# Two of Linear's four blocks turned by block loads and VectorE in place of TensorE, and the order of their pieces

## The chip, the cores and the metric

One core of one Trainium2 chip runs the whole program in one launch. The metric is the device time in microseconds (us) of that launch. The program is bound to one order of instructions on each of its engines when it is built: TensorE (PE in the profile) multiplies, VectorE (DVE), ScalarE (ACT) and GpSimd (POOL) work on elements, and SyncE (SP) issues nearly all transfers between HBM and the on-chip SBUF, one after the other. Engines wait for one another on semaphores; an engine takes its instructions strictly in order, so what waits holds all that stands behind it.

## What is computed

The input `x` has 2 sequences of 1024 tokens, 512 wide, in float32. Four layers follow, each with a residual and a layernorm after it:

```python
x = _layernorm(x + _L0_attn_ref(x, ...))   # Mamba-like recurrent layer, inner width 1024
x = _layernorm(x + _L0_ffn_ref(x, ...))    # ternary linear layer, here called Linear
x = _layernorm(x + _L1_attn_ref(x, ...))   # gated linear recurrence (RG-LRU) with a short convolution
x = _layernorm(x + _L1_ffn_ref(x, ...))    # SwiGLU with weights stored as integers
```

The change lies in the second layer, at its border with the first and the third:

```python
out = jnp.einsum('bln,nk->blk', x, weight) * scale      # weight is -1, 0 or 1
v_norm = jnp.maximum(jnp.linalg.norm(out, axis=-1, keepdims=True), EPS)
out = out * (jnp.tanh(v_norm) / (v_norm + EPS))
o_norm = jnp.maximum(jnp.linalg.norm(out, axis=-1, keepdims=True), EPS)
out = out * jnp.minimum(0.99 / o_norm, 1.0)
```

## The kernel before

The 2048 tokens are cut into four blocks of 512 (`NBLK = 4`, `TB = 512`), and a block's rows into four tiles of 128 tokens (`NJ = 4`); the 512 features are four tiles of 128 as well (`NK = 4`). A block in rows, tokens on the partitions, is `X[b]`; each layer's products want it turned, features on the partitions. Line numbers are those of the kernel before.

The first layer works block by block. Its last step for a block is `conclude`: for each row tile `j` eight matmuls `po` (L770, in two halves of four, each 128x128 by 128x512 in float32) give the output rows, and VectorE adds them, times `rms`, to `X[b]` (L785, printed `x<-po,rms,x`). The `rms` come from sums of squares that `gate` makes before: ACT squares (L757), and POOL adds seven of them up into `sums` (L759). The squares live in temporary buffers of the first layer's pool, which is given back when they are done with. The finished blocks are normalised and stored to HBM in rows as `x_mid[b]`, blocks 0 to 2 well before the stretch that matters here, and block 3 inside it.

`later_layers` opens two pools in the space that the first layer gives back: `ep` (tiles of the second and fourth layer) and `wp` (the third layer's weights, tags w0 to w4). A tile that takes space over from others waits for whoever last used that space. Then it issues its loads on SP, in this order: `w_f0` (Linear's weight, L900), `X[0]` and `X[1]` in rows from `x_mid` (L903), Linear's scale (L99), `w_x` and `w_y` (L909), `X[2]` (L910), the parameters (L93, L861), and later `w_ig`, `w_ag` and the fourth layer's integer weights (L927).

`linear(b)` is a generator that does the Linear layer for block `b`, in four steps divided by `yield`:

1. turn the block and split it in two parts, a rounded one and the rest (`split`), so that the product with the ternary weight is exact in TensorE's fast format. Blocks 0, 1 and 2 are turned by `transposed`: sixteen PE transposes (L237) into four PSUM banks, ACT's cast (L241) of each bank and DVE's subtraction (L244). Block 3 (`mid`) is turned by `load_blocks` and `turn_blocks`: four DMAs (L265) bring `x_mid[3]` from HBM in pieces of 32 floats, placed so that 32x32 blocks only have to be transposed in themselves, and DVE does that with four instructions (L273), after which ACT casts (L955) and DVE subtracts (L957).
2. eight matmuls (L987, four features by two parts) for each of two row tiles, and for each DVE's multiplication by the scale into `o` (L991) and ACT's sum of squares (L993);
3. the same for the other two row tiles;
4. the tail: ACT and DVE make the factor `f` from the norms (L997 to L1009), DVE adds `o` times `f` to the rows (L1011, `x<-o,f,x`), takes the layernorm's statistics (L283, L286, reciprocal L289), and POOL normalises the rows (L291; for block 0 DVE takes the last of the four rows). Blocks 1 to 3 are stored as `x_lin[b]`.

The order around it is made by `weave(main, fill, plan)`, which takes `plan[i]` steps of `fill` after step `i` of `main`. conclude of block 3 has eight steps, two for each row tile, and a last one with its layernorm and store; linear(0) and linear(1) are its fill:

```python
weave(steps, itertools.chain(linear(0), linear(1)), (0, 1, 0, 2, 0, 1, 0, 2, 1))
```

Then comes the third layer. `branches(0)` turns the finished `x0` with sixteen PE transposes (L237, evicted by ACT at L249 into a tile in slot w4) and multiplies it with `w_x` and `w_y` (L1069); linear(2) is woven into it with `(1,) * 4`, and linear(3) into the gates that follow. From there the third layer and the fourth run as before and after.

The tile framework has a scheduler: within what the data and the buffers allow, it may move an instruction in its engine's order by priority. `tc.keep_in_program_order(...)` holds one instruction behind the one that was written just before it on its engine; others may still be moved past either.

`parameters()` also computes a softplus of `a_param` on DVE and ACT (L213 to L224), some twenty small instructions on 128x4 elements which the scheduler strews between others.

Of the kernel before, what the change touches and what calls it, by code (L numbers as in the profile page):

```python
# [9 lines left out]
F32 = mybir.dt.float32  # L10
# [3 lines left out]
ALU = mybir.AluOpType  # L14
PSUM = bass.MemoryType.PSUM

P = 128
TB = 512
NJ = TB // P
D = 512  # L20
NK = D // P
# [16 lines left out]
def model_kernel(ctx: ExitStack, tc: tile.TileContext, t: dict, out: bass.AP):  # L38
    nc = tc.nc
    ctx.enter_context(nc.allow_non_contiguous_dma(reason="small parameter columns"))  # L40
    BATCH, SEQ, _ = t["L0_attn_hidden_states"].shape
    NBLK = BATCH * SEQ // TB
# [3 lines left out]
    x_mid = tc.dram_tile([NBLK, TB, D], F32, name="x_mid")  # L46
# [35 lines left out]
    X = [tokens() for _ in range(3)]  # L82
# [49 lines left out]
    w_out = op.tile([P, NX, D], F32, tag="w_out", name="w_out")  # L132
# [90 lines left out]
        nc.vector.tensor_scalar(r, z, 0.0, None, ALU.max)  # L223
        nc.vector.scalar_tensor_tensor(o, p, 2.0, r, ALU.mult, ALU.add)  # L224

    def transposed(pool, b, X, tags=("xT",), split=False, bufs=1, by_act=False, behind=False, soon=False):


        pieces = [
            pool.tile([P, NK, TB], F32R if split else F32, tag=tag, name=f"{tag}{b}", bufs=bufs)  # L230
            for tag in tags
        ]
        xT = pieces[0]
        for k in range(NK):
            pt = bank("pt")
            for j in range(NJ):
                nc.tensor.transpose(  # L237
                    pt[:, j * P : (j + 1) * P], X[b][:, j, k * P : (k + 1) * P], ident
                )
            if split:  # L240
                copied = nc.scalar.copy(xT[:, k, :], pt)  # L241
                if behind:
                    tc.keep_in_program_order(copied)
                nc.vector.tensor_tensor(  # L244
                    pieces[1][:, k, :], pt, xT[:, k, :].bitcast(F32), ALU.subtract
                )
            elif soon:
                with tc.high_priority():
                    nc.scalar.copy(xT[:, k, :], pt)  # L249
            elif k % 2 or by_act:  # L250
                nc.scalar.copy(xT[:, k, :], pt)
            else:
                nc.vector.tensor_copy(xT[:, k, :], pt)
        return pieces
# [6 lines left out]
    def load_blocks(dst, rows, pinned=False):  # L261

        blocks = rows.rearrange("(n t) (k a c) -> a t k n c", t=32, k=NK, c=32)
        for a in range(4):
            load = nc.sync.dma_start(  # L265
                dst[32 * a : 32 * a + 32].rearrange("t k (n c) -> t k n c", c=32), blocks[a]
            )
            if pinned:
                tc.keep_in_program_order(load)

    def turn_blocks(dst, src=None, pinned=False):
        for k in range(NK):
            turned = nc.vector.transpose(dst[:, k, :], (src or dst)[:, k, :])  # L273
            if pinned:
                tc.keep_in_program_order(turned)
# [28 lines left out]
    def weave(main, fill, plan, rest=True):  # L304

        for i, _ in enumerate(main):
            for _ in range(plan[i] if i < len(plan) else 0):
                next(fill, None)
        for _ in fill if rest else ():
            pass  # L310
# [451 lines left out]
    def conclude(b, st):  # L762


        xc, sums = st["xc"], st["sums"]
        rms = sp.tile([P, NJ], F32, tag="rms", name="rms")
        for j in range(NJ):
            po = bank("po")
            for m in range(NX):
                nc.tensor.matmul(  # L770
                    po, xc[:, m, j * P : (j + 1) * P], w_out[:, m, :],
                    start=(m == 0), stop=(m == NX - 1),
                )
                if m == NX // 2 - 1:
                    yield
            if j == 0:
                pss = bank("pss")
                for i in range(NJ):
                    nc.tensor.matmul(
                        pss[:, i : i + 1], sums[:, i * P : (i + 1) * P], ones,  # L780
                        start=True, stop=True,
                    )
                nc.scalar.activation(rms, pss[:, :NJ], AF.Sqrt, bias=eps, scale=1.0 / DI)
                nc.vector.reciprocal(rms, rms)
            nc.vector.scalar_tensor_tensor(  # L785
                X[b][:, j, :], po, rms[:, j : j + 1], X[b][:, j, :], ALU.mult, ALU.add
            )
            yield
        if b:
            layernorm(X[b], pinned=b == NBLK - 1)  # L790
            store_rows(x_mid[b], X[b])
# [93 lines left out]
    def later_layers(exact, last=None):  # L885
# [4 lines left out]
        X = Y  # L890
# [8 lines left out]
        w_f0 = ep.tile([P, NK, D], F32, tag="wF", name="w_f0" + suffix)  # L899
        nc.sync.dma_start(w_f0, w_f0_source)  # L900
        rows_mid = [x_mid[b].rearrange("(j p) d -> p j d", p=P) for b in range(NBLK)]
        for b in range(2):
            nc.sync.dma_start(X[b], rows_mid[b])  # L903
        w1 = [
            wp.tile([P, NK, D], F32, tag=f"w{i}", name=f"w1{i}{suffix}") for i in range(4)
        ]
# [41 lines left out]
            wf = ep.tile([P, NK, D], F32, tag="wg0", name="wfg")  # L948
            nc.vector.tensor_copy(wf, w_f0)

        def split(x, pieces):


            for k in range(NK):
                nc.scalar.copy(pieces[0][:, k, :], x[:, k, :])  # L955
                if exact:
                    nc.vector.tensor_tensor(  # L957
                        pieces[1][:, k, :], x[:, k, :], pieces[0][:, k, :].bitcast(F32),
                        ALU.subtract,
                    )  # L960
# [7 lines left out]
        def linear(b):  # L968

            tags = ("wu0", "wd0") if exact else ("wu0",)  # L970
            if b == NBLK - 1:
                turn_blocks(mid)
                w1.append(wp.tile([P, NK, D], F32, tag="w4", name="w14" + suffix))
                xT = [ep.tile([P, NK, TB], WT, tag=tag, name=f"{tag}{b}") for tag in tags]
                split(mid, xT)
                nc.sync.dma_start(w1[4], w_sources["w_out"])
            else:

                xT = transposed(ep, b, X, tags=tags, split=exact, behind=b == 2)
            yield  # L980
            o = ep.tile([P, NJ, D], F32, tag="wF", name="o" + suffix)
            ssq = sp.tile([P, NJ], F32, tag="ssq", name="ssq")
            for j in range(NJ):
                po = bank("po")
                for k in range(NK):
                    for x in xT:
                        nc.tensor.matmul(  # L987
                            po, x[:, k, j * P : (j + 1) * P], wf[:, k, :],
                            start=(k == 0 and x is xT[0]), stop=(k == NK - 1 and x is xT[-1]),
                        )  # L990
                nc.vector.tensor_tensor(o[:, j, :], po, f0s, ALU.mult)  # L991
                junk = ep.tile([P, GW], mybir.dt.bfloat16, tag="junk", name="junk2")
                nc.scalar.activation(junk, o[:, j, :], AF.Square, accum_out=ssq[:, j : j + 1])  # L993
                if j % 2:
                    yield
            norm = sp.tile([P, NJ], F32, tag="norm", name="norm")
            nc.scalar.activation(norm, ssq, AF.Sqrt)  # L997
            v = sp.tile([P, NJ], F32, tag="v", name="v")
            nc.vector.tensor_scalar(v, norm, 1e-7, None, ALU.max)
            f = sp.tile([P, NJ], F32, tag="f", name="f")  # L1000
            nc.scalar.activation(f, v, AF.Tanh)
            nc.vector.tensor_scalar(v, v, 1e-7, None, ALU.add)
            nc.vector.reciprocal(v, v)
            nc.vector.tensor_tensor(f, f, v, ALU.mult)
            nc.vector.tensor_tensor(norm, norm, f, ALU.mult)
            nc.vector.tensor_scalar(norm, norm, 1e-7, None, ALU.max)
            nc.vector.reciprocal(norm, norm)
            nc.vector.tensor_scalar(norm, norm, 0.99, 1.0, ALU.mult, ALU.min)
            nc.vector.tensor_tensor(f, f, norm, ALU.mult)  # L1009
            for j in range(NJ):  # L1010
                nc.vector.scalar_tensor_tensor(  # L1011
                    X[b][:, j, :], o[:, j, :], f[:, j : j + 1], X[b][:, j, :],
                    ALU.mult, ALU.add,
                )
            layernorm(X[b], engine=nc.gpsimd, last=None if b else nc.vector)
            if b:
                store_rows(x_lin[b], X[b])
            yield

        if last:  # L1020
            steps, free = last

            weave(steps, itertools.chain(linear(0), linear(1)), (0, 1, 0, 2, 0, 1, 0, 2, 1))
            free()
        else:
            for _ in itertools.chain(linear(0), linear(1)):
                pass
        for i, name in ((2, "w_ig"), (3, "w_ag")):
            nc.sync.dma_start(w1[i], w_sources[name])
# [28 lines left out]
        with tc.tile_pool(name="rec" + suffix, bufs=1, side="right", reuse_waits="tile") as rp:  # L1058
# [125 lines left out]
                yield  # L1184

            st = {}
            weave(branches(0, st), linear(2), (1,) * 4)
            lin = [coming_block(1)]
            bout = row("L1_attn_b_out", D, c1, nc.sync, "scale")
            ys = []  # L1190
# [254 lines left out]
```

## Time and profile before

| | us |
|---|---|
| median of 3 runs | 1117.68 |
| lowest and highest | 1117.55, 1117.88 |
| the profiled execution | 1116.89 |
| its span, first to last instruction | 1115.1 |
| PE busy | 1099.4 (99%) |
| DVE busy | 701.4 (63%) |
| ACT busy | 451.4 (40%) |
| POOL busy | 366.8 (33%) |
| PE at conclude's products (L770, 256) | 112.5 |

The granted clock of PE is 0.998 in the mean. "Busy" is time in which an engine has an instruction under way; for PE the ends of the pipelined matmuls are modelled. In lists of the profile a line reads: start, length, engine, line of the kernel, operation, output<-inputs by the program's names, and in brackets how long the engine was idle before it and what ended that. "SPq" is the issue of a transfer in SP's queue, not the transfer. A list of waits reads: who <- what it waited for: us in total, times, longest.

### The profile page before, as it was taken

What the parts mean: (1) busy time and instruction counts of PE and PEld (TensorE: products, weight loads), DVE (VectorE), ACT (ScalarE), POOL (GpSimd) and SP (SyncE); (2) the same over time, 40 slices, a digit from 0 to 9 for tenths busy, and PEclk for the clock granted to TensorE, in tenths of its full rate; (3) what the DMA queues carried; (4) which work ended last, traced back from release to release, by engine and by line L of the source; (5) the groups of instructions that cost most, each with busy time, mean ns of one, the idle gap of its engine ahead of it and who ended that gap; (6) DMA issues with size and microseconds to landing.
All of it is one profiled execution on the core that took longest, in us unless ns stands there. A gap on an engine that the chain in (4) does not pass through costs nothing.

```text
span 1115.1 us, 12073 instructions
## 1 busy us (share of the span) xinstructions
PE 1099.4 (99%) x4450; PEld 663.3 (59%) x4450; DVE 701.4 (63%) x1267; ACT 451.4 (40%) x690; POOL 366.8 (33%) x347
## 2 busy tenths in 40 slices
PE   8999999999999999999999999999999999999996
PEld 5455445445544555745444444447888888888885
DVE  5989797797869676875727437184238866325224
ACT  3334624463454233556653372553223224224223
POOL 1547471565348240254433231236511001001000
PEclk9999999999999999999999999999999999999999
DMA  8005200911210137245650001304544002100001
GB/s 323 21 9 126 91 1 17 253 30 39 105 81 0 39 135 215 57 94 123 113 113 37 1 1 49 27 0 143 189 94 76 1 1 63 14 1 30 8 1 41
DMA packets 122059, 77.04 MB, mean 69 GB/s; under 512 B 94512, under 2 KB 95312, under 8 KB 120456
## 3 DMA queue, kind: packets, MB, share of 16 engines
q1 hardware_dynamic: 120792, 75.77, 25.7%
q8 instruction: 37, 0.61, 0.2%
q10 hardware_dynamic: 976, 0.39, 0.1%
q14 instruction: 30, 0.25, 0.1%
q0 software_dynamic: 224, 0.02, 0.0%
HBM read 59.95 MB, written 16.02 MB: 68 GB/s over the span
## 4 chain that ended last, share of the span: by engine, by line
PE 80%; DVE 11%; ACT 4%; issue 2%; POOL 2%; DMA 1%; SPq 0%; DVEq 0%; ACTq 0%; POOLq 0%
PE pgu L1039 20%; PE p L1069 16%; PE po L1270 10%; PE pg L372 9%; PE px L372 7%; PE po L770 6%; DVE acc L298 3%; PE po L1159 2%; PE py L705 2%; DVE L L578 2%; PE po L987 2%; PE pxt L674 1%; PE pt L237 1%; POOL x L1165 1%; PE py L697 1%
## 5 line engine op out<-in xcount | busy, mean ns | idle before, releaser
L1050 DVE SCALAR_TENSOR_TENSOR h<-pgu,L_ffn_up_scale,sg 128x512 f32<-128x512 f32 x63 | 47.1, 748 | 126.4 <-PE pgu L1039 122.6
L372 PE MATMUL px<-xT,w_in 128*128 128x512 f32 x256 | 114.6, 597 | 0.0
L593 POOL TENSOR_TENSOR L<-L,gm 128x512 f32<-128x512 f32 x64 | 93.5, 1490 | 63.7 <-DVE bdec L588 34.7
L372 PE MATMUL pg<-xT,w_in 128*128 128x512 f32 x256 | 113.5, 594 | 0.0
L770 PE MATMUL po<-w_out,xc 128*128 128x512 f32 x256 | 112.5, 593 | 0.7 <-DVE L L578 0.7
L1069 PE MATMUL p<-cv,w 128*128 128x512 f32 x256 | 110.8, 592 | 0.0
L1039 PE MATMUL pgu<-wF__4239,wg 128*128 128x512 f32 x256 | 101.7, 397 | 0.0
L1039 PE MATMUL pgu<-lo__4240,wg 128*128 128x512 f32 x256 | 100.8, 394 | 0.0
L1039 PE MATMUL pgu<-lo__4240,wu 128*128 128x512 f32 x256 | 100.7, 393 | 0.0
L1039 PE MATMUL pgu<-wF__4239,wu 128*128 128x512 f32 x256 | 100.7, 393 | 0.0
L1270 PE MATMUL po<-wd,hh 128*128 128x512 f32 x252 | 98.3, 396 | 0.3 <-POOL wg L930 0.3
L1270 PE MATMUL po<-wd,hl 128*128 128x512 f32 x252 | 98.3, 396 | 0.2 <-DVE hl L1054 0.2
L1049 ACT ACTIVATE sg<-pgu,L_ffn_gate_scale 128x512 f32<-128x512 f32 x63 | 43.4, 689 | 127.6 <-PE pgu L1039 127.6
L770 PEld LDWEIGHTS po<-w_out,xc 128*128 128x128 f32 x256 | 48.4, 190 | 61.8 <-issue 56.7
L1053 ACT CAST hh<-h 128x512 fp32r<-128x512 f32 x63 | 39.1, 621 | 112.5 <-DVE h L1050 112.3
L1069 PEld LDWEIGHTS p<-cv,w 128*128 128x128 f32 x256 | 48.6, 190 | 60.4 <-issue 58.8
L1069 PE MATMUL p<-xT,w 128*128 128x512 f32 x192 | 82.9, 592 | 0.0
L372 PEld LDWEIGHTS px<-xT,w_in 128*128 128x128 f32 x256 | 47.5, 190 | 57.5 <-issue 55.5
L298 DVE SCALAR_TENSOR_TENSOR acc<-xpad,cols,acc 128x512 f32<-128x512 f32 x72 | 68.5, 953 | 20.0 <-ACT acc L342 15.2
L372 PEld LDWEIGHTS pg<-xT,w_in 128*128 128x128 f32 x256 | 47.3, 190 | 54.2 <-issue 53.1
L1386 POOL TENSOR_TENSOR x<-x,r 128x512 f32<-128x512 f32 x12 | 15.2, 1295 | 195.0 <-DVE r L1385 195.0
L578 DVE TENSOR_TENSOR_SCAN L<-pl,id 128x512 f32<-128x512 f32 x64 | 75.0, 1205 | 4.7 <-ACT pl L572 3.7
(292 smaller groups left out, 1921.9 us busy)
## 6 DMA issues: line engine op xcount, KB each, us to landing
L<-decays SPq DMA_DIRECT2D x12, 1024.0 KB, 8.0
x_mid<-x SPq DMA_DIRECT2D x4, 1024.0 KB, 4.3
x<-x_mid SPq DMA_DIRECT2D x4, 1024.0 KB, 7.5
st<-in_L_ffn_gate_w_dram SPq DMA_DIRECT2D x8, 512.0 KB, 6.4
st<-in_L_ffn_up_w_dram SPq DMA_DIRECT2D x8, 512.0 KB, 4.4
st<-in_L_ffn_down_w_dram SPq DMA_DIRECT2D x8, 512.0 KB, 3.8
x_rec<-x SPq DMA_DIRECT2D x4, 1024.0 KB, 4.3
x<-_attn_hidden_states_dram SPq DMA_DIRECT2D x3, 1024.0 KB, 16.8
```

The costliest lines, as they stand in the source:

```text
L298: tap = nc.vector.scalar_tensor_tensor(acc, xpad[:, k : k + TB], w[:, k : k + 1], acc, ALU.mult, ALU.add)
L372: nc.tensor.matmul(pm[:n, :], w_in[:, k, lo : lo + n], xT[:, k, :], start=(k == 0), stop=(k == NK - 1),)
L578: nc.vector.tensor_tensor_scan(L[:, h, :], pl, id4.rearrange("p j t -> p (j t)"), 0.0, ALU.mult, ALU.add)
L593: nc.gpsimd.tensor_tensor(L[:, h, :], L[:, h, :], st["gm"], ALU.mult)
L705: nc.tensor.matmul(pys[i][hh * HD : (hh + 1) * HD, q, :], dtx[q][:, 2 * i + hh, :], L[:, h, s], start=(first and q == 0), stop=(q == 1), s ...
L770: nc.tensor.matmul(po, xc[:, m, j * P : (j + 1) * P], w_out[:, m, :], start=(m == 0), stop=(m == NX - 1),)
L1039: nc.tensor.matmul(pm, w[g][:, k, cols], x[:, k, :], start=(k == 0 and x is pieces[0]), stop=(k == NK - 1 and x is pieces[-1]),)
L1049: nc.scalar.activation(sg, pgu[0], AF.Silu, scale=gs[:, m : m + 1])
L1050: nc.vector.scalar_tensor_tensor(h, pgu[1], us[:, m : m + 1], sg, ALU.mult, ALU.mult)
L1053: nc.scalar.copy(halves[0], h)
L1069: nc.tensor.matmul(pm, w1[i][:, k, m * P : (m + 1) * P], rhs[:, k, :], start=(k == 0), stop=(k == NK - 1),)
L1270: nc.tensor.matmul(po[j], x[:, j * P : (j + 1) * P], wd[m // GK][:, m % GK, :], start=(m == 0 and x is h[0]), stop=(m == NF - 1 and x is h ...
```

## The change

linear(1) and linear(2) are turned as linear(3) was: two new tiles, `raw1` (in `wp`, tag w4, and the first tile of that pool) and `raw2` (in `ep`, tag lo) are loaded with `load_blocks` from `x_mid[1]` and `x_mid[2]`, turned in place by DVE's `turn_blocks`, and split from SBUF. raw1's four DMAs are issued between `w_f0` and the rows of `X[0]`; raw2's four come after the rows of `X[1]`. The 2 x 16 PE transposes of these blocks go.

The order changes too. `first_two()` interleaves the steps of linear(0) (`one`), linear(1) (`two`) and linear(2) (`third`): the first step of a block stands in front of the last step (the tail) of its neighbour. The first step of linear(2) has a `yield` of its own between the turns and the split. Three steps in place of two are taken after conclude's row tile 1 (the third is linear(1)'s turn and split). linear(2) has its first two steps there (turns and split), and the rest is woven into `branches(0)`, beginning one step later, with `(0, 1, 1, 1)`. Held behind the instruction written before them are: conclude's evictions of row tiles 1 and 2 of the last block, the turns of blocks 1 and 2, the casts of block 2, and the instruction `v` (maximum with 1e-7) of linear(1). The argument `behind` of `transposed` goes.

```diff
@@ -223,7 +223,7 @@
         nc.vector.tensor_scalar(r, z, 0.0, None, ALU.max)
         nc.vector.scalar_tensor_tensor(o, p, 2.0, r, ALU.mult, ALU.add)
 
-    def transposed(pool, b, X, tags=("xT",), split=False, bufs=1, by_act=False, behind=False, soon=False):
+    def transposed(pool, b, X, tags=("xT",), split=False, bufs=1, by_act=False, soon=False):
 
 
         pieces = [
@@ -238,9 +238,7 @@
                     pt[:, j * P : (j + 1) * P], X[b][:, j, k * P : (k + 1) * P], ident
                 )
             if split:
-                copied = nc.scalar.copy(xT[:, k, :], pt)
-                if behind:
-                    tc.keep_in_program_order(copied)
+                nc.scalar.copy(xT[:, k, :], pt)
                 nc.vector.tensor_tensor(
                     pieces[1][:, k, :], pt, xT[:, k, :].bitcast(F32), ALU.subtract
                 )
@@ -782,9 +780,12 @@
                     )
                 nc.scalar.activation(rms, pss[:, :NJ], AF.Sqrt, bias=eps, scale=1.0 / DI)
                 nc.vector.reciprocal(rms, rms)
-            nc.vector.scalar_tensor_tensor(
+            sum_ = nc.vector.scalar_tensor_tensor(
                 X[b][:, j, :], po, rms[:, j : j + 1], X[b][:, j, :], ALU.mult, ALU.add
             )
+            if b == NBLK - 1 and 0 < j < NJ - 1:
+
+                tc.keep_in_program_order(sum_)
             yield
         if b:
             layernorm(X[b], pinned=b == NBLK - 1)
@@ -899,8 +900,17 @@
         w_f0 = ep.tile([P, NK, D], F32, tag="wF", name="w_f0" + suffix)
         nc.sync.dma_start(w_f0, w_f0_source)
         rows_mid = [x_mid[b].rearrange("(j p) d -> p j d", p=P) for b in range(NBLK)]
+
+        def untouched(b, pool, tag):
+
+            x = pool.tile([P, NK, TB], F32, tag=tag, name=f"raw{b}" + suffix)
+            load_blocks(x, x_mid[b])
+            return x
+
+        raw = [untouched(1, wp, "w4")]
         for b in range(2):
             nc.sync.dma_start(X[b], rows_mid[b])
+        raw.append(untouched(2, ep, "lo"))
         w1 = [
             wp.tile([P, NK, D], F32, tag=f"w{i}", name=f"w1{i}{suffix}") for i in range(4)
         ]
@@ -948,11 +958,13 @@
             wf = ep.tile([P, NK, D], F32, tag="wg0", name="wfg")
             nc.vector.tensor_copy(wf, w_f0)
 
-        def split(x, pieces):
+        def split(x, pieces, pinned=False):
 
 
             for k in range(NK):
-                nc.scalar.copy(pieces[0][:, k, :], x[:, k, :])
+                cast = nc.scalar.copy(pieces[0][:, k, :], x[:, k, :])
+                if pinned:
+                    tc.keep_in_program_order(cast)
                 if exact:
                     nc.vector.tensor_tensor(
                         pieces[1][:, k, :], x[:, k, :], pieces[0][:, k, :].bitcast(F32),
@@ -968,15 +980,19 @@
         def linear(b):
 
             tags = ("wu0", "wd0") if exact else ("wu0",)
-            if b == NBLK - 1:
-                turn_blocks(mid)
-                w1.append(wp.tile([P, NK, D], F32, tag="w4", name="w14" + suffix))
+            if b:
+                x = mid if b == NBLK - 1 else raw.pop(0)
+                turn_blocks(x, pinned=b < NBLK - 1)
+                if b == 2:
+                    yield
+                if b == NBLK - 1:
+                    w1.append(wp.tile([P, NK, D], F32, tag="w4", name="w14" + suffix))
                 xT = [ep.tile([P, NK, TB], WT, tag=tag, name=f"{tag}{b}") for tag in tags]
-                split(mid, xT)
-                nc.sync.dma_start(w1[4], w_sources["w_out"])
+                split(x, xT, pinned=b == 2)
+                if b == NBLK - 1:
+                    nc.sync.dma_start(w1[4], w_sources["w_out"])
             else:
-
-                xT = transposed(ep, b, X, tags=tags, split=exact, behind=b == 2)
+                xT = transposed(ep, b, X, tags=tags, split=exact)
             yield
             o = ep.tile([P, NJ, D], F32, tag="wF", name="o" + suffix)
             ssq = sp.tile([P, NJ], F32, tag="ssq", name="ssq")
@@ -996,7 +1012,10 @@
             norm = sp.tile([P, NJ], F32, tag="norm", name="norm")
             nc.scalar.activation(norm, ssq, AF.Sqrt)
             v = sp.tile([P, NJ], F32, tag="v", name="v")
-            nc.vector.tensor_scalar(v, norm, 1e-7, None, ALU.max)
+            least = nc.vector.tensor_scalar(v, norm, 1e-7, None, ALU.max)
+            if b == 1:
+
+                tc.keep_in_program_order(least)
             f = sp.tile([P, NJ], F32, tag="f", name="f")
             nc.scalar.activation(f, v, AF.Tanh)
             nc.vector.tensor_scalar(v, v, 1e-7, None, ALU.add)
@@ -1017,13 +1036,22 @@
                 store_rows(x_lin[b], X[b])
             yield
 
+        third = linear(2)
+
+        def first_two():
+
+            one, two = linear(0), linear(1)
+            for steps in (one, one, one, two, one, third, two, two, third, two):
+                next(steps)
+                yield
+
         if last:
             steps, free = last
 
-            weave(steps, itertools.chain(linear(0), linear(1)), (0, 1, 0, 2, 0, 1, 0, 2, 1))
+            weave(steps, first_two(), (0, 1, 0, 3, 0, 1, 0, 2, 1))
             free()
         else:
-            for _ in itertools.chain(linear(0), linear(1)):
+            for _ in first_two():
                 pass
         for i, name in ((2, "w_ig"), (3, "w_ag")):
             nc.sync.dma_start(w1[i], w_sources[name])
@@ -1184,7 +1212,7 @@
                 yield
 
             st = {}
-            weave(branches(0, st), linear(2), (1,) * 4)
+            weave(branches(0, st), third, (0, 1, 1, 1))
             lin = [coming_block(1)]
             bout = row("L1_attn_b_out", D, c1, nc.sync, "scale")
             ys = []
```

## Prediction

> **What bounds the kernel now.** I read the page's busy shares first, then the chain of waits over the stretch that the change touches (395 to 515 us), then the queues that feed PE there.
>
> ```profile
> PE 1099.4 (99%) x4450; PEld 663.3 (59%) x4450; DVE 701.4 (63%) x1267; ACT 451.4 (40%) x690; POOL 366.8 (33%) x347
> PEclk9999999999999999999999999999999999999999
> ```
>
> PE is busy for 1099.4 of 1115.1 us, at full clock. Work taken from PE is time saved, and any wait put in front of PE is time lost: no idle time is there to absorb it. The chain (start, length, what) through the last conclude and the Linear blocks:
>
> ```profile
> 408.93 6.87 PE po L770 x16
> 415.79 0.79 PE pss L779 x8
> 416.58 1.81 PE pt L237 x16
> 418.38 6.87 PE po L770 x16
> 425.25 7.30 PE po L987 x32
> 432.56 13.73 PE po L770 x32
> 446.29 1.75 PE pt L237 x16
> 448.04 7.47 PE po L987 x32
> 455.51 3.49 PE pt L237 x32
> 459.00 3.44 PE p L1069 x8
> ```
>
> No gap anywhere. L770 is conclude's product, L987 Linear's, L237 the transposes: block 0's at 416.58, block 1's at 446.29, and at 455.51 thirty-two, namely 16 of the finished x0 (branch 0's input) and then 16 of block 2. Two deadlines matter below: PE wants x0's raw rows at 416.58, and x0's finished rows after linear(1), at 455.51.
>
> SP's queue (start, length in the queue, what) shows when the rows come:
>
> ```profile
> 408.96 0.91 SPq L903 DMA_DIRECT2D x<-x_mid  x2
> 409.92 0.50 SPq L99 DMA_DIRECT2D L_ffn_scale<-in_L_ffn_scale_dram  x1
> 415.40 0.37 SPq L909 DMA_DIRECT2D w<-in_L_attn_w_x_dram  x1
> ...
> SPq L903 <- PE pg L372: 6.6, 1, 6.6
> SPq L909 <- POOL sums L759: 5.0, 1, 5.0
> ```
>
> x0 and x1 leave at 408.96. The next big load, w_x into slot w0, waits 5.0 us for conclude's last sums on POOL (L759, seven adds from 404.06, 11.31 us long, to 415.37): that slot lies where the last squares are.
>
> DVE and POOL (same columns) close x0 for its second deadline:
>
> ```profile
> 438.91 0.16 DVE L1009 TENSOR_TENSOR f<-f,norm 128x4 f32<-128x4 f32 x1
> 439.11 0.75 DVE L1011 SCALAR_TENSOR_TENSOR x<-o,f,x 128x512 f32<-128x512 f32 x1
> 442.43 1.28 DVE L283 BATCH_NORM_STATS2 st<-x 128x6 f32<-128x512 f32 x2
> 446.33 0.75 DVE L785 SCALAR_TENSOR_TENSOR x<-po,rms,x 128x512 f32<-128x512 f32 x1 [1.09 <-PE po L770]
> 447.34 6.48 POOL L291 TENSOR_SCALAR x<-x,mv,rs 128x512 f32<-128x512 f32 x3 [31.96 <-PE pt L237]
> ```
>
> linear(0)'s whole tail (L999 to L1011, the statistics) ran beside conclude's last products, and was done before their last eviction at 446.33. POOL's three rows ended at 453.8, 1.7 us ahead of PE's need.
>
> **The change, part by part.** All is reckoned against the profiled execution, 1116.89 us (span 1115.1 and 1.8 around it), 0.8 under the median of 1117.68; less than 0.2% (2.2 us) could not be told from no change.
>
> *Removed.* Blocks 1 and 2's transposes: 1.75 us at 446.29, and half of the 3.49 at 455.51. Both are on PE's chain: **−3.5 us**.
>
> *Split from SBUF instead of PSUM.* Four casts of 0.62 us on ACT (L955) in place of 0.60 (L241); four subtractions of 0.69 on DVE (L957) in place of 0.68 (L244). Nothing. The eight turns cost DVE 8 × 0.62 = 5.0 us (mid's four took 2.49); block 1's hide under conclude's 13.73 us of products, and block 2's are priced below.
>
> *Block loads moved ahead of x0 on SP: stall A.* raw1 is now the first tile of its pool (tag w4), so it takes the space over the last squares that w0 had, and inherits the wait for POOL's sums: its first DMA leaves at 415.4. SP issues in order, and x0's load stands behind raw1's four: it can't leave at 408.96 any more. The nearest row for raw1, with queues empty before it, is the block load of x_rec:
>
> ```profile
> 693.87 5.62 SPq L265 DMA_DIRECT2D rec<-x_rec  x4
> GB/s 0 0 0 0 0 0 0 0 0 72 185 207 148 133 124 123 124 142 138 124 124 119 116 29 0 0 0 0 0 0 0 0 0 0 0 0 0 0 0 0
> ```
>
> The second line is the DMA view of 690 to 712 us in slices of 0.55: data flow until 703.0, 9.1 us after the issue, in 128-byte pieces at some 125 GB/s. The row load of X[3] behind mid's four block loads (issued 487.67, landed 7.0 us later) came 2.4 us after mid's last block had landed, so rows wait for the blocks ahead of them. For x0: 415.4 + 9.1 + 2.7 (1 MB at the 380 GB/s of row loads) + about 1 us to the landing = 428.2; by the other count, 415.4 + 5.6 + 7.0 = 428.0. PE stands at L237 from 416.58, and everything behind it in PE's order waits: **+11.5 us**. Low end: issue at 415.4 + 5.6 and 5.3 us for a row load with nothing ahead, as x0's took before, 426.3, +9.7. High end: the block load of lin1 took 8.75 us of SP (8.75 + 7.0 → 431.2): +14.6. raw2 stands behind x0 and x1, and is wanted some 30 us later. w_x, w_y, the Linear scale and the ten parameters are pushed back some 20 us. The scale would land near 440, where linear(0)'s first product, shifted, ends near 438.7: evictions slip a little, PE has banks enough. Nothing.
>
> *DVE's order: stall B.* The built order puts conclude's last eviction (L785, j = 3) ahead of linear(0)'s tail after v, and right behind it the turns of raw2, which are pinned to it. DVE waits there for PE's last L770 product. So the tail that hid under 13.73 us of products starts only when they are over. From that moment, on DVE: eviction 0.7; raw2's four turns 2.4; the small chain L1002 to L1009 1.6 (437.48 to 439.11); four x<-o 2.7; four statistics 2.8 (442.43 to 445.24); some dozen small steps of the softplus between them 1.2; two evictions and a statistic of linear(1) 1.8; reciprocal and hand-over 0.4; 13.6 in all. Then POOL's three rows, 6.4: 20.0 us. PE has linear(1), 7.5 us, to cover it, and then stands at x0's transposes: **+12.5 us**. If all fillers were free, 17.0 and +9.5; with each of 13 small steps at its full 0.19 us and the turns at 0.67, 21.6 and +14.1.
>
> *Block 2's transposes as cover.* ACT's evictions of x0's transposes (four of 0.60) ran under them; now the first L1069 product waits for the last of those: **+0.8** (0.5 to 1.2).
>
> *Clock.* Two idle spells of over 11 us are new. Only the ends of this run have such: after the last matmul (ended 1106.4) the granted clock is 0.52 from 1111 on, and at the start L188's first 17 matmuls took 3.77 us, twice the time per matmul of the later ones. So I take 1.9 us for each spell (3.8 us at half rate), **+3.8**; from 0 (at the end the clock still reads 1.00 from 1106 to 1111, so some 4.7 us of idleness did not lower it) to twice that.
>
> The Trainium skill ("TensorE: Matmul & The Clock Gate", Part 1, on the HAM clock gate, and Part 4) gives about 3.4 us of idleness to halve the clock and as much busy time to restore it, and says that transposes don't count as busy. Both stalls end at 16 transposes; by that rule these would run at half rate and not start the warming, 1.75 us more for each, and the sum would be 3.5 higher. No row here shows transposes on a cold clock, and I stay with the 1.9.
>
> *Weave and linear(2) made earlier.* The same matmuls in another order. x_mid[3]'s store and mid's load keep their place behind PE's transposes and shift with them; the chain of 472 to 502 us (POOL, DVE and ACT beside a busy PE) shifts whole. Nothing, with ±1.
>
> Sum: −3.5 + 11.5 + 12.5 + 0.8 + 3.8 = **+25.1**: 1142.0 profiled, 1142.8 for a median. Its own range: 1117.68 − 3.5 + 9.7 + 9.5 + 0.5 = 1134 to 1117.68 − 3.5 + 14.6 + 14.1 + 1.2 + 7.6 = 1152.
>
> **Rivals.**
>
> *Only stall B.* raw1's loads leave at once, because the wait for the sums falls elsewhere; if they leave by 404, x0 lands by 416.6 (12.7 later) and A is gone. For: SP is idle before 408.96. Against: the pool puts its first tile where L909's wait came from. −3.5 + 12.5 + 0.8 + 1.9 = +11.7, 1129.4.
>
> *Only stall A.* x0's rows are finished within linear(1)'s 7.5 us in spite of the order, since DVE and POOL run the tail more densely than before. For: L291's rows cost DVE 0.54 us, POOL 2.1. Against: POOL's three rows alone use 6.4 of the 7.5, and the x<-o and the statistics, 5.5, come before them. −3.5 + 11.5 + 0.8 + 1.9 = +10.7, 1128.4.
>
> *Faster.* Rows and tail both come in time, and PE keeps just what it gave up: −3.5 + 0.8 = −2.7, 1115.0. It is decided at L237's two places, x0's rows by 416.6 and POOL's last row by the end of linear(1), 453.8 on the new count. For: before, both had about 2 us to spare. Against: both orders above, which I read from the built queues.
>
> *No change.* A single short wait of 2 to 4 us that returns the 3.5.
>
> **How the numbers follow.** Both stalls 0.78; only B 0.09; only A 0.07; faster 0.05; no change 0.01. So faster 0.05, same 0.01, slower 0.94. The forecast is the first case's 1142.8. Its own range keeps some 0.66; for 8 in 10 the range goes down to the one-stall cases, a little under them: 1127 to 1152.
>
> **What would show it.** After: 64 transposes at L237 in place of 96; raw1's issue at 415.4 behind POOL's sums, x0's near 421; PE idle some 11.5 us in front of block 0's transposes, ended by the DMA x<-x_mid; a second idle spell near 12 us in front of x0's finished rows, ended by POOL's L291; the clock's tenths low in two slices between 400 and 500 us; the FFN's stretches unchanged in length. Without the first gap, or with x0's load ahead of raw1, stall A was wrong; if POOL's rows begin less than 10 us after the last L770 product, stall B was. A total under 1117 means that neither was on PE's path.

## The result and the profile after

The changed kernel takes 1141.87 us (median of 5 runs, 1141.49 to 1142.89), the kernel before 1117.55: the ratio is 1.0221, its 95% interval 1.0208 to 1.0234. The profiled execution of the changed kernel took 1142.89 us, its span is 1140.8, 25.7 longer than before's. The page first:

```profile
PE 1102.9 (97%) x4418; PEld 664.4 (58%) x4418; DVE 705.3 (62%) x1275; ACT 449.1 (39%) x688; POOL 366.9 (32%) x347
PEclk9999999999999988799999999999999999999999
```

PE has 32 instructions fewer (64 transposes in place of 96) and is busy 3.5 us longer, since some of its work ran on a halved clock: slices 15 to 17, that is 400 to 485 us. The chain of waits over that stretch (start, length, what; line numbers of the changed kernel: L768 is conclude's product, L1003 Linear's, L237 the transposes, L263 a block load, L289 the layernorm's rows):

```profile
415.43 0.64 SPq L263
...
421.01 7.63 DMA x<-x_mid
...
428.78 3.65 PE pt L237 x16
432.42 7.67 PE po L768 x16
440.10 7.30 PE po L1003 x32
447.40 13.75 PE po L768 x32
...
461.84 1.29 DVE raw L271 x2
...
473.91 2.36 POOL x L289
476.27 4.11 POOL x L289 x2
```

Before, this stretch was PE from end to end. Now the chain leaves PE twice: once through POOL's sums, SP's four block loads and x0's transfer, and once, from conclude's last product to the finished x0, through DVE and POOL. The largest of PE's own waits (who <- for what: us, times, longest) are these; the next, 1.4 us, lies at the program's start, in both kernels:

```profile
PE pt L237 <- DMA x<-x_mid: 12.2, 1, 12.2
PE pt L237 <- POOL x L289: 9.3, 2, 7.9
PE pt L237 <- POOL xpad L1120: 1.6, 1, 1.6
```

The third belongs to the second: POOL's xpad is what POOL did right after x0's last row. Three of x0's transposes ran between these waits, as its rows came one by one. SP's queue (start, length, what) and, below it, DVE and POOL around conclude's last eviction (L783):

```profile
415.43 5.54 SPq L263 DMA_DIRECT2D raw<-x_mid  x4
421.01 2.40 SPq L912 DMA_DIRECT2D x<-x_mid  x2
...
461.18 0.75 DVE L783 SCALAR_TENSOR_TENSOR x<-po,rms,x 128x512 f32<-128x512 f32 x1 [6.04 <-PE po L768]
...
465.56 1.42 DVE L1030 SCALAR_TENSOR_TENSOR x<-o,f,x 128x512 f32<-128x512 f32 x2
...
473.91 6.47 POOL L289 TENSOR_SCALAR x<-x,mv,rs 128x512 f32<-128x512 f32 x3 [58.51 <-DVE sp L222]
```

x0's load leaves at 421.0 and not at 409. DVE stands idle for 6.04 us at the eviction, with linear(0)'s whole tail behind it, and POOL's rows begin 12.7 us after it.

### The profile page after: what moved, and what is told of

It is laid out like the page before. It is cut to its first block, busy times and chain, and to the rows that moved or that the text cites. A ratio compares the mean times of both kernels' runs of the same rounds, so it can differ in the third digit from the quotient of the medians.

```text
span 1140.8 us, 12031 instructions
## 1 busy us (share of the span) xinstructions
PE 1102.9 (97%) x4418; PEld 664.4 (58%) x4418; DVE 705.3 (62%) x1275; ACT 449.1 (39%) x688; POOL 366.9 (32%) x347
## 4 chain that ended last, share of the span: by engine, by line
PE 75%; DVE 13%; ACT 4%; POOL 3%; issue 2%; DMA 2%; SPq 1%; DVEq 0%; ACTq 0%; POOLq 0%
PE pgu L1067 20%; PE p L1097 15%; PE po L1298 10%; PE pg L370 8%; PE px L370 6%; PE po L768 5%; DVE acc L296 3%; PE po L1187 2%; DVE L L576 2%; PE py L703 2%; PE po L1003 1%; DVE xc L753 1%; POOL x L289 1%; PE pxt L672 1%; DVE st L281 1%
## 5 line engine op out<-in xcount | busy, mean ns | idle before, releaser
L768 PE MATMUL po<-w_out,xc 128*128 128x512 f32 x256 | 113.4, 596 | 0.7 <-DVE L L576 0.7
L1097 PE MATMUL p<-cv,w 128*128 128x512 f32 x256 | 110.8, 592 | 0.0
L768 PEld LDWEIGHTS po<-w_out,xc 128*128 128x128 f32 x256 | 48.8, 192 | 62.3 <-issue 57.5
L1097 PEld LDWEIGHTS p<-cv,w 128*128 128x128 f32 x256 | 48.6, 190 | 60.4 <-issue 58.4
L1097 PE MATMUL p<-xT,w 128*128 128x512 f32 x192 | 82.9, 592 | 0.0
```

The lines of the kernel that those rows point to most:

```text
L768: nc.tensor.matmul(po, xc[:, m, j * P : (j + 1) * P], w_out[:, m, :], start=(m == 0), stop=(m == NX - 1),)
L1097: nc.tensor.matmul(pm, w1[i][:, k, m * P : (m + 1) * P], rhs[:, k, :], start=(k == 0), stop=(k == NK - 1),)
```

## Experiments

**The order of the loads (e1).** Only the loads are moved:

```diff
-        raw = [untouched(1, wp, "w4")]
         for b in range(2):
             nc.sync.dma_start(X[b], rows_mid[b])
+        f0s = par["f0s"] = row("L0_ffn_scale", D, c1, nc.sync, "scale")
+        raw = [untouched(1, wp, "w4")]
         raw.append(untouched(2, ep, "lo"))
...
-        f0s = par["f0s"] = row("L0_ffn_scale", D, c1, nc.sync, "scale")
```

> The rows of X[0] and X[1] and Linear's scale are loaded ahead of raw1 and raw2, nothing else is edited. Theory: the 12.2 us in front of block 0's transposes come from x0 standing behind raw1 on SP, so x0 leaves at 409 again, lands near 414, and the first stall with its cold clock (2.6 us) goes. The built order of DVE changes with it: linear(0)'s tail now stands ahead of conclude's last eviction, so the second stall (12 us and some 2 us of cold clock) shrinks to 2 us or less too. The time would then be 1142 - 14.8 - 12 = 1115 if nothing new comes; since block 2's turns now stand behind block 3's layernorm on DVE, I expect new waits of 4 to 9 us in front of linear(2) and linear(3): 1119 to 1125. Rival: the block loads themselves crowd the queues and DVE has too much to do whatever the order; then x0 lands late or its rows are finished late all the same, and the time stays above 1130.

Measured: 1125.54 us, ratio 1.0075 (1.0057 to 1.0093). The chain, and PE's waits in this stretch and behind it:

```profile
417.10 1.81 PE pt L237 x16
418.91 6.87 PE po L768 x16
...
PE po L1003 <- ACT wu L965: 5.5, 2, 3.8
PE pt L237 <- POOL x L289: 1.2, 1, 1.2
PE po L1003 <- DVE wd L969: 1.2, 1, 1.2
```

That is just above the 1119 to 1125 expected. The first stall is gone, and the second is down to 1.2 us with no edit to DVE: in this build linear(0)'s tail stands ahead of conclude's last two evictions. So the order of the loads on SP lies behind both stalls. The likely reason is that the scheduler orders DVE's work by when it takes the data to be there; no run shows that, and since the scale moved with the rows, which of the two it went by is open. In their place come 6.7 us of waits in front of linear(2) and linear(3), since block 2's turns stand behind block 3's layernorm on DVE.

**Order or space (e4).** The same order of loads and of DVE, but raw1 in other space:

```diff
-        raw = [untouched(1, wp, "w4")]
...
         w1 = [
             wp.tile([P, NK, D], F32, tag=f"w{i}", name=f"w1{i}{suffix}") for i in range(4)
         ]
+        raw = [untouched(1, wp, "w4")]
```

> The weights' four tiles are taken from the pool before raw1, so raw1 lies in other space (behind w3, where the last squares were not) while the order of all loads on SP and of DVE is that of the changed kernel. Theory: the first stall comes from the wait for POOL's sums that raw1 inherits with its space, not from the order or the transfers: raw1 leaves right behind w_f0, near 402 to 403, x0 at 409, landing near 416 to 418; the first stall is 0 to 2 us and its clock stays warm, while the second stays at 12 us: 1142 - 11 - 2.6 = 1128. Rival: eight block loads in 128-byte pieces are what delays x0; then x0 lands after 420 and less than 8 us are won: 1134 or more.

Measured: 1130.78 us, ratio 1.0118 (1.0100 to 1.0137). SP's queue, then PE's waits:

```profile
403.01 8.72 SPq L263 DMA_DIRECT2D raw<-x_mid  x4
411.78 2.40 SPq L915 DMA_DIRECT2D x<-x_mid  x2
...
PE pt L237 <- POOL x L289: 9.2, 2, 7.9
PE pt L237 <- DMA x<-x_mid: 2.0, 1, 2.0
```

raw1 leaves 12.4 us earlier, still ahead of x0, and 10.2 of the 12.2 us of the first stall go. The wait that raw1 inherited with its space was the cause; the block loads ahead of x0 cost 2.0 us by themselves. The second stall stays with x0 only 2 us late, so it follows from the order that was built, not from how late x0 really is. The forecast of 1128 was 2.8 us too low: 2.0 us of the stall stayed, and the first transposes still ran on a slow clock (below).

**The last eviction held behind linear(0)'s tail (e2).** The loads as in the changed kernel:

```diff
-            if b == NBLK - 1 and 0 < j < NJ - 1:
+            if b == NBLK - 1 and 0 < j:
```

> Conclude's eviction of row tile 3 is held behind linear(0)'s tail too (0 < j in place of 0 < j < NJ - 1); the loads stay as in the changed kernel. Theory: the first stall stays at 12.2 us. x0's statistics run under conclude's products again, but the reciprocal in front of POOL's rows is built behind three evictions of linear(1), so the second stall only shrinks, from 12 us to some 6.5: 1142 - 5.5 = 1136.5, up to 1142 if the work moved comes late in front of linear(3). Rival: the second stall is POOL's and not DVE's; then it keeps its 12 us and the time is 1142.

Measured: 1147.77 us, ratio 1.0276 (1.0257 to 1.0294), slower than the changed kernel, where 1136 to 1142 was expected. PE's waits, besides the 11.9 us of the first stall:

```profile
PE p L1097 <- ACT ga L1155: 8.4, 1, 8.4
PE pt L237 <- POOL x L289: 4.1, 2, 2.6
PE pt L237 <- POOL xpad L1120: 1.6, 1, 1.6
```

The second stall shrank from 10.9 to 5.7 us about as foreseen, POOL's rows being the same; so DVE's order and not POOL's speed made the rest of it. What was not foreseen is a new wait of 8.4 us some 85 us later, in the third layer. The list puts it down to ACT, which alternates there between the gates' sigmoids (L1151) and exponentials (L1154), with a table load of 1.28 us at each turn. To test that (e7), the first exponential was held in its place:

```diff
-                    nc.scalar.activation(al[:, m, :], ga[:, m, :], AF.Exp, scale=sneg[:, m : m + 1])
+                    decay = nc.scalar.activation(
+                        al[:, m, :], ga[:, m, :], AF.Exp, scale=sneg[:, m : m + 1]
+                    )
+                    if b == 0 and m == 0:
+                        tc.keep_in_program_order(decay)
```

> As e2_last_pinned, and one more instruction held in the written order: the first exponential of the first recurrence block on ACT behind the four sigmoids written before it. Theory: e2's 1147.8 in place of 1136.5 is an 8.4 us wait of PE in the third layer for ACT, which alternated between sigmoids and exponentials and loaded a table of 1.28 us each time; the pin takes that away, 1147.8 - 8.4 = 1139.4, with the second stall at 5.7 us as in e2. Rival: the shifted work of DVE is what makes ACT late; then the wait stays in some form and the time is over 1144.

Measured: 1136.35 us, ratio 1.0174 (1.0158 to 1.0189). The wait for ACT is gone from the list, but ACT was not its cause. Its table loads around these gates are seven in e2, and seven in before and in the changed kernel too, where PE doesn't wait; in e7 they are still six, and ACT needs 19.5 us from the first sigmoid to the last tanh, against 18.5 in e2. What differs is DVE's order. PE's next products (L1097) multiply block 1, which DVE has to turn first (L271). DVE in e2, in the changed kernel and in e7:

```profile
546.33 0.18 DVE L287 RECIPROCAL rs<-rs 128x4 f32<-128x4 f32 x1 [1.70 <-ACT rs L286]
555.94 0.06 DVE L1172 MEMSET al<- 128x1 f32 x1 [9.43 <-POOL a L1159]
556.08 2.49 DVE L271 STREAM_TRANSPOSE xT<-lin 128x512 f32<-128x512 f32 x4
...
552.38 0.18 DVE L287 RECIPROCAL rs<-rs 128x4 f32<-128x4 f32 x1 [1.70 <-ACT rs L286]
552.55 2.49 DVE L271 STREAM_TRANSPOSE xT<-lin 128x512 f32<-128x512 f32 x4
...
545.61 2.49 DVE L271 STREAM_TRANSPOSE xT<-lin 128x512 f32<-128x512 f32 x4
```

In e2 the turn was built behind a small write (L1172) that waits 9.43 us for POOL, and PE starts at 556.94, as the first of the four turns ends. In the other two it stands right behind the reciprocal. ACT's last tanh ended at the same moment in e2, which would explain why the list names ACT; in the changed kernel PE starts these products at 554.42, over 8 us before it. The pin on ACT changed the order built for DVE; no run moved the turn alone.

The gain over e2, 11.4 us, is 3 more than the wait itself. Behind the wait PE ran some 3 us at a granted clock of 0.50 in e2, which costs 1.5, and the transposes and products behind the first stall took 11.03 us there and 10.38 in e7.

**The clock (e5, e6).** Products of the identity with itself on PE in front of block 0's transposes, 100 of them, and in a second kernel 50:

```diff
+                warm = bank("warm")
+                for _ in range(100):
+                    tc.keep_in_program_order(
+                        nc.tensor.matmul(warm[:, :P], ident, ident, start=True, stop=True)
+                    )
                 xT = transposed(ep, b, X, tags=tags, split=exact)
```

> 100 products of the identity with itself, 128x128, into a bank that nobody reads, are put on PE in front of block 0's transposes, that is, into the first stall; the rest is the changed kernel. They add no data. Theory: at 0.11 us each they fill 11 of the 12.2 us, the stall itself stays as x0 is not earlier, but the clock stays at full rate: block 0's transposes take 1.8 us and not 3.65, the next products 6.9 and not 7.7: 1142 - 2.6 = 1139.2. Rival: the slow transposes come from something else (rows arriving piecewise, SBUF traffic); then the time is the same, 1142, or a little more.

Measured: 1151.28 us, ratio 1.0303 (1.0285 to 1.0322). The size was wrong: each product is two instructions of 0.11 us, so the hundred took 22.4 us and outlasted the stall.

```profile
417.73 22.44 PE warm L998 x200
440.17 1.75 PE pt L237 x16
```

Behind them transposes and products run at full speed, but x0 had long been there. With 50:

> As e5_warm, with 50 products in place of 100: each of those showed as two records of 0.112 us and 100 of them took 22.4 us, so 50 take 11.2 and fit into the first stall of 12.2. Theory: the stall stays, as x0 lands no earlier, but PE meets it on a full clock: block 0's transposes take 1.8 us and not 3.65, and the next products 6.9 and not 7.7: 1142 - 2.6 = 1139.2. Rival: the transposes were slow because the rows came in piece by piece; here they come as late as in the changed kernel, so the transposes stay slow and the time 1142.

Measured: 1141.48 us, ratio 1.0222 (1.0207 to 1.0238), where 1139.2 was expected. The chain:

```profile
421.24 8.62 DMA x<-x_mid
...
429.99 1.94 PE pt L237 x16
431.93 6.87 PE po L768 x16
```

The rows come as late as before, and yet the transposes take 1.94 us and not 3.65, the products 6.87 and not 7.67. So the slow transposes were the clock. The 2.5 us won show only in part in the total (1141.58 profiled against 1142.89; the medians are only 0.4 apart): x0's transfer took 8.62 us here and 7.63 in the changed kernel, so PE began 1.2 later. In two other kernels with the same loads it took 7.33 and 7.39. Why it varies is open.

**Both blocks without the stalls (e9).** Rows and scale ahead of raw1 and raw2 as in the first experiment, the first exponential held as in e7, and:

```diff
-            for steps in (one, one, one, two, one, third, two, two, third, two):
+            for steps in (one, one, one, two, one, two, third, two, third, two):
...
-            layernorm(X[b], engine=nc.gpsimd, last=None if b else nc.vector)
+            layernorm(X[b], engine=nc.gpsimd if b else nc.vector, last=nc.vector)
```

> A try with both blocks turned by block loads: rows and scale ahead of raw1 and raw2, the steps taken in the order one, one, one, two, one, two, third, two, third, two (block 2's turns in front of block 3's layernorm and not behind it), x0's rows and one in four of the others on DVE, the first exponential pinned. Theory: 3.5 us of transposes go; 0.8 comes back for ACT's evictions without cover; linear(2)'s first products are paced by its subtractions on DVE, some 3 us, and linear(3)'s come 1.5 late: 1117.5 - 3.5 + 0.8 + 4.4 = 1119. Rival: with the loads out of the way nothing is late, 1115.

Measured: 1118.37 us against 1117.01 of before run beside it, ratio 1.0017 (1.0008 to 1.0026). PE's waits in the same stretch:

```profile
PE po L1003 <- DVE wd L969: 2.4, 4, 0.8
PE po L1003 <- ACT wu L965: 1.3, 1, 1.3
```

The 3.5 us of transposes are saved, and 3.7 come back in front of linear(2) and linear(3): with both blocks turned and split from SBUF, DVE delivers linear(2)'s parts at its own pace. That alone would be level; where the other 1.2 us lie was not traced.

**Block 1 alone (e8).** As in the last kernel, but block 2 keeps its PE transposes inside the first branch:

```diff
-            if b:
+            if b in (1, NBLK - 1):
                 x = mid if b == NBLK - 1 else raw.pop(0)
...
-            for steps in (one, one, one, two, one, third, two, two, third, two):
+            for steps in (one, one, one, two, one, two, two, two):
...
-            weave(branches(0, st), third, (0, 1, 1, 1))
+            weave(branches(0, st), third, (1,) * 4)
```

raw2's load and the pins on conclude's evictions and on v are left out too.

> A try at a faster kernel. Only block 1 is turned by block loads; block 2 keeps its PE transposes, woven into the first branch as before, so they still cover ACT's evictions of x0. The rows of X[0], X[1] and the scale are loaded ahead of raw1; linear(1)'s turn still stands in front of linear(0)'s tail; the pins on conclude's evictions and on v go; all four rows of x0 are normalised on DVE and one row in four of the others; the first exponential is pinned as in e7. Theory: 1.75 us of transposes go, and about half a microsecond of waits stays: 1117.5 - 1.2 = 1116.3. Rival: even one block's turns and the rows on DVE make linear(2) or linear(3) late by more than the 1.75: 1118 to 1121.

Measured: 1115.41 us against 1117.01 of before run beside it, ratio 0.9986 (0.9977 to 0.9995): a little faster than the kernel before. The chain is PE's again, without the 1.75 us of block 1:

```profile
432.57 13.73 PE po L768 x32
446.31 7.30 PE po L999 x32
453.61 3.49 PE pt L237 x32
```

Its side edits alone, on the kernel before (e10: the rows on DVE and the held exponential, the diffs shown above):

> A control for e8_block1: the kernel before with e8's two side edits alone, all four rows of x0 and one row in four of the other blocks normalised on DVE, and the first exponential of the recurrence held in the written order; all transposes stay on PE. If e8's 1.6 us come from block 1's transposes (1.75 us of PE), this kernel takes the time of before, 1117.0 (0 to 1 us more, where DVE's extra rows delay linear(1)). Rival: e8 was faster for its side edits; then this kernel gains the same, 1115.4.

Measured: 1118.06 us against 1117.61, ratio 1.0004 (0.9995 to 1.0013). They bring nothing. With e8's chain, which is shorter by just the 1.75 us of block 1's transposes, that puts the 1.6 us down to these; the new order of steps and loads was not run by itself.

## Why the prediction came out

The forecast was 1142.8, with 25.1 us over before; 24.3 were measured in the medians. By its own terms, from the two chains:

| term | predicted | measured |
|---|---|---|
| 32 transposes fewer | −3.5 | −3.5 |
| stall A, x0's raw rows | +11.5 | +12.2 (416.58 to 428.78) |
| stall B, x0's finished rows | +12.5 | +11.3 (468.44, the end of linear(1)'s last product, to 480.44, less 0.7 for three transposes in it) |
| ACT's evictions uncovered | +0.8 | 0 |
| clock | +3.8 | +5.3 |
| sum | +25.1 | +25.3 (spans: +25.7) |

The cause and the path were as forecast. That the sum came so close is in part luck: its terms were off by +0.7, −1.2, −0.8 and +1.5, which nearly cancel.

**Stall A** was right in cause and size: raw1's first DMA left at 415.43, x0's at 421.01, its rows landed at 428.64 (forecast 415.4, 421.0 and 428.0 to 428.2). e4 shows the inherited wait to be 10 of the 12 us.

**Stall B** was right in its place and mechanism. From conclude's last product to POOL's first row took 12.8 us, not 13.6. What the prediction lacked is why DVE was ordered so; e1 shows that the order follows from that of the loads on SP, and moving x0's rows and the scale ahead takes both stalls nearly away. The rival "only stall B" is nearly e4, where raw1's wait falls elsewhere: 1129.4 was its price, 1130.78 was measured.

**The cover** term was mis-sized, +0.8 against nothing. The prediction let the first product wait for the last of ACT's four evictions, and it doesn't: it starts at 483.27, as the transposes end, and the last eviction begins only at 483.88. In e1, with the transposes at full clock, it is the same: 457.16 and 457.54.

**The clock** term was mis-sized the other way. Behind stall A the transposes took 3.65 in place of 1.81 and the next products 7.67 in place of 6.87, 2.6 us; behind stall B some 1.8 for the transposes and 0.9 for the first eight products, 2.7. The row that priced it, the start of the program, has 3.8 us at half rate, as read from the length of its matmuls (the clock column says 1.00 there); here it was about 5.

The prediction weighed a statement of the Trainium skill ("TensorE: Matmul & The Clock Gate", Part 4) that transposes don't count as busy for the clock, by which each cold spell would last through the 16 transposes and for a whole warming after them. The runs speak against it. Behind the first stall of e7 (start:end, length, PE busy, granted clock, then DMA):

```profile
428.44:431.95 3.51, 3.51 (x17) 0.54 1.16 290
431.95:438.82 6.87, 6.87 (x17) 1.00 1.56 137
```

The clock is at full rate as soon as the 16 transposes are over, with no product behind them; in the changed kernel it came 1.5 us later than that. Staying with the row from the trace was right, though 0.7 too low for each stall.

**The rivals**: "faster" needed both deadlines met; e8 meets them, for one block, and gets 1.6 us. What the transposes are worth, 1.75 us a block, was right.

## What to carry to other kernels

A tile that is allocated first in a new pool takes the space, and the wait, of whatever lay there: look at what is queued behind its load on the same engine before asking what the load itself costs. Where a scheduler orders the engines, moving one load can reorder another engine's work, and a pin in one place cost 8 us some 85 us later, where a turn was built behind another engine's wait; so read the built order of every engine, not only the edited one. A wait is put down to whatever ended last: before blaming that, look whether the same work stands, without the wait, in a kernel that is fast. When the bound engine is 99% busy, taking work from it pays at most that work (1.75 us a block here), while each new wait costs its full length and the clock on top.

## What the hardware showed that was not expected

A short gap can be enough to halve PE's clock. In e4 PE idled only 2.0 us, behind eight single-column products (L777, 0.9 us), and the next 3.5 us ran at about half rate (windows of e4: start:end, length, PE busy, granted clock, then DMA):

```profile
416.30:417.20 0.90, 0.87 (x9) 1.00 1.06 389
417.20:419.20 2.00, 0.03 (x1) 0.96 1.04 383
419.20:422.70 3.50, 3.50 (x17) 0.54 1.14 262
422.70:430.00 7.30, 7.30 (x20) 1.00 1.47 145
```

The prediction's bound, that 4.7 us of idleness at the program's end left the clock at 1.00, would not have allowed this. The length of the gap does not settle it alone: in e6 PE idled 1.9 us behind its 100 filling instructions, and the clock stayed at 1.00:

```profile
429.99:431.93 1.94, 1.94 (x17) 1.00 1.36 211
```

Whether the single-column products of e4 count as idle is not shown. The length of the slow spell behind a stall varied between runs of the same mechanism, from 3.5 us (e4, e7) to about 5 (the changed kernel); what sets it was not tried.
